# SS2D block on one Trainium2 core: the output stage with channels on partitions, norms and residuals by products on TensorE

## Chip, cores and metric

One NeuronCore of a Trainium2 chip. The time is the device time of one execution of the whole program, in microseconds (us).

## The reference

Four layers run one after the other on x of shape (8, 56, 56, 128) in float32. Layers 0, 2 and 3 are deformable convolutions with a small MLP; they are not touched. Layer 1 is a visual state-space block (SS2D). For each image, with Di = 256 inner channels and L = 56 x 56 = 3136 positions:

```python
xn = _ln(x, norm1_w, norm1_b)
xz = jnp.einsum('bhwc,ec->bhwe', xn, in_proj_w)
xx, z = jnp.split(xz, 2, axis=-1)
# xx: depthwise 3x3 convolution and silu; then a selective scan in four directions (K = 4, N = 16 states)
h = h * jnp.exp(dt_t[..., None] * A) + (dt_t * u_t)[..., None] * B_t[:, :, None, :]
# y: the sum of the four directions' outputs
y = _ln(y, out_norm_w, out_norm_b)
y = y * jax.nn.silu(z)
y = jnp.einsum('bhwd,cd->bhwc', y, out_proj_w)
x = x + y
xm = _ln(x, norm2_w, norm2_b)
h = jax.nn.gelu(jnp.einsum('bhwc,fc->bhwf', xm, fc1_w) + fc1_b)
x = x + jnp.einsum('bhwf,cf->bhwc', h, fc2_w) + fc2_b
```

`_ln` subtracts the mean over the channels, divides by the root of the variance plus 1e-5, and applies a weight and a bias for each channel. The lines from `y = _ln(...)` to the end are what the kernel calls the output stage.

## The kernel before

Class `Vss` computes layer 1. Its inner loop (`scans`) goes over 8 images, 4 directions in the order 1, 3, 0, 2, and 4 chunks of 784 positions: 128 steps. A step has 32 *units*; a unit holds 32 channels x 4 states on the 128 partitions and 784 positions on the free axis, so there are 4096 units. Each unit does the following:

- ACT: `decay`, the exponential dA (L1346), into one of two PSUM buffers.
- DVE: `inputs`, the product u of b and dtu (L1356) in three units of four; in the fourth, POOL does it as up (L1352). dtu is a copy of dt*x that PE spreads into PSUM (`spread`, L1340) once for each four units; it has one buffer.
- DVE: the scan itself (L1449), from dA and u to h.
- POOL: hc = h*c (L1454).
- PE: the sum of hc over the states into acc (L1378), opened at L1370 and closed by copies on ACT (L1389).

Beside the units two kinds of further work are emitted. `prepare` makes the next step's dt, b and c; one of its parts goes out every second unit. *Tasks* form a queue of generators: the input stage of the next image (norm, in-projection, nine-tap convolution as 18 products of 448 columns a chunk, seven chunks an image) and the output stages of an image, eight of them, each for SH = 392 positions. `advance(1)` runs the first task in the queue up to its next `yield`. It is called in 24 of 32 units (odd t, or t a multiple of 4), and in every unit while the last image is in its last direction. An output stage is queued when the last direction closes its chunk, two at a time. What is still queued after the last scan runs by itself; layer 2 follows it. `prepare`, the input stage and the output stage all take their PSUM from one bank, `misc`, with one buffer. Each engine works its own queue in order, and all loads and stores go through SP's queue.

The output stage before (L1159 to L1230, 28 yields) takes y with channels on partitions and goes over to positions on partitions: n = 98 positions in T = 4 groups.

- L1162 and L1164 load y (yin) and the gate sg, each 128 x 2 x 392.
- L1173: eight transposes on PE, two groups at a time. `stats` (L1062) takes BATCH_NORM_STATS2 (L1069) and BATCH_NORM_AGGREGATE (L1070) on DVE from PSUM; Ln and Exp (L204, L205) make the inverse root, and small ACT operations (L1073, L1074) the negated product with the mean. `normalize` (L1080) writes z on ACT.
- L1186: eight transposes back (L1090); ACT applies weight and bias as it copies to gT (L1187). POOL multiplies by sg (L1189).
- L1195: the projection, eight products with positions on the output's partitions. DVE adds the input rows xt (L1198).
- Statistics and normalization again, from xt; four transposes (L1090); ACT writes xT with weight and bias (L1208).
- fc1 (L1213), four products of 392 columns, each copied out by ACT with its bias (L1214); gelu with a table load ahead of it and one behind it (L1216, L1218); fc2 (L1224), 16 products on top of a bias row (L298).
- DVE adds xt (L1227); L1229 stores the rows.

A float32 product shows as two records of the profile on PE; a transpose shows as one.

Of the kernel before, what the change touches and what calls it, by code (L numbers as in the profile page):

```python
# [41 lines left out]
F32 = mybir.dt.float32  # L42
BF16 = mybir.dt.bfloat16
I32 = mybir.dt.int32
AF = mybir.ActivationFunctionType
# [5 lines left out]
NIMG, H, W, C = 8, 56, 56, 128  # L51
# [60 lines left out]
DI, NST, NDIR, RANK = 256, 16, 4, 8  # L112
NCH = DI // 128
XD = RANK + 2 * NST

LC = 448
# [4 lines left out]
SH = SC // 2  # L121

FF = 512
NF = FF // 128
# [16 lines left out]
def bcast(ap, axis, n):  # L141
    shape = list(ap.shape)
    shape.insert(axis, n)
    return ap.unsqueeze(axis).to_broadcast(shape)
# [845 lines left out]
class Vss:  # L990
# [27 lines left out]
    def weights(self):  # L1018
# [34 lines left out]

        w["sum"] = self.cp.tile([128, TC], F32, name="v_sum", tag="v_sum")
# [39 lines left out]
    def input_stage(self, i):  # L1094
# [34 lines left out]
        for c in range(NLC):  # L1129
# [7 lines left out]
            z = self.bg.tile([128, T, C], F32, name="z", tag="z", padded_shape=[128, T, DI])  # L1137
# [20 lines left out]

    def output_stage(self, i, c):  # L1159
# [7 lines left out]
        z = self.bg.tile([128, T, DI], F32, name="z", tag="z")  # L1167
        for t0 in range(0, T, 2):
            ps = self.misc()
            for t in range(2):  # L1170
                at = n * (t0 + t)
                for ch in range(NCH):
                    nc.tensor.transpose(ps[:n, DI * t + 128 * ch : DI * t + 128 * (ch + 1)], y[:, ch, at : at + n], self.net.ident)  # L1173
            yield
            yield
            srcs = [ps[:n, DI * t : DI * (t + 1)] for t in range(2)]
            rs = self.stats(srcs)
            yield
            self.normalize(z[:, t0 : t0 + 2], srcs, rs)
            yield  # L1180
        xt = self.bg.tile([128, T, C], F32, name="xt", tag="xt", bufs=2)
        nc.sync.dma_start(out=xt[:n], in_=self.rows_of(self.src[i], c, n))
        gT = self.bg.tile([128, NCH, m], F32, name="gT", tag="gT")
        for ch in range(NCH):
            ps = self.misc()
            self.transpose(ps, [z[:n, t, 128 * ch : 128 * (ch + 1)] for t in range(T)])  # L1186
            nc.scalar.activation(gT[:, ch, :], ps[:, :m], AF.Identity, bias=w["now_b"][:, ch : ch + 1], scale=w["now_w"][:, ch : ch + 1])  # L1187
            yield
        nc.gpsimd.tensor_mul(gT, gT, sg)  # L1189
        yield  # L1190
        yield
        po = self.misc()
        for t in range(T):
            for ch in range(NCH):
                nc.tensor.matmul(po[:n, 128 * t : 128 * (t + 1)], lhsT=gT[:, ch, n * t : n * (t + 1)], rhs=w["out"][:, ch, :], start=ch == 0, stop=ch == NCH - 1)  # L1195
        yield
        yield
        nc.vector.tensor_add(xt[:n], xt[:n], po[:n].rearrange("p (t c) -> p t c", c=128))  # L1198
        srcs = [xt[:n, t, :] for t in range(T)]
        rs = self.stats(srcs)  # L1200
        yield
        z = self.bg.tile([128, T, C], F32, name="z", tag="z", padded_shape=[128, T, DI])
        self.normalize(z, srcs, rs)
        yield
        ps = self.misc()
        self.transpose(ps, [z[:n, t, :] for t in range(T)])
        xT = self.bg.tile([128, m], F32, name="xT", tag="xT")
        nc.scalar.activation(xT, ps[:, :m], AF.Identity, bias=w["n2b"], scale=w["n2w"])  # L1208
        yield
        pre = self.bg.tile([128, NF, m], F32, name="pre", tag="pre", padded_shape=[128, NF, LC])  # L1210
# [11 lines left out]
        for t in range(T):  # L1222
            for f in range(NF):
                nc.tensor.matmul(po[:n, 128 * t : 128 * (t + 1)], lhsT=pre[:, f, n * t : n * (t + 1)], rhs=w["fc2"][:, f, :], start=False, stop=t == T - 1 and f == NF - 1)  # L1224
            if t % 2:
                yield
        nc.vector.tensor_add(xt[:n], xt[:n], po[:n].rearrange("p (t c) -> p t c", c=128))  # L1227
# [316 lines left out]
```

## Time and profile before

| | us |
|---|---|
| median of 3 runs | 18470.5 (18470.23 to 18477.48) |
| span of the profiled execution | 18479.8 |
| first to last scan (L1449) | 2365 to 13799 |
| last output stage ends | about 14015 |
| DVE busy | 15510.8 (84%) |
| POOL busy | 11801.5 (64%) |
| ACT busy | 11145.4 (60%) |
| PE busy | 13780.6 (75%) |

Of the profiled execution the trace gives its span and no other time. A row of a group of instructions reads: line, engine, operation, output<-input by the program's names, partitions x elements, count | busy us in all, mean ns of one | idle us of the engine just before them, and who ended that idle time. A row of a window gives, for each engine, its busy us and the number of its instructions in brackets, then the granted clock of TensorE as a share of full speed, the busy share of the DMA engines and GB/s. PEld is the load of weights, which runs beside PE. Matmuls are pipelined and their ends are modelled, so a busy PE is not a full one. A row of the timeline begins with its start and its length in us.

### The profile page before, as it was taken

How to read it: one execution, taken by the hardware profiler on the slowest of the kernel's cores; microseconds unless marked ns; L12 is line 12 of the kernel's file. 1: busy time of each engine (PE TensorE's matmuls, PEld its weight loads, DVE VectorE, ACT ScalarE, POOL GpSimd, SP SyncE). 2: the span in 40 equal slices, each digit the busy share in tenths (PEclk: the TensorE clock that was granted, in tenths of full speed). 3: DMA queues.
4: the chain of work that ended last, by engine and by line, in shares of the span. 5: the costliest groups of instructions: out<-in, count | busy, mean ns of one | idle time of the engine just before them, and what ended most of it. 6: DMA issues, size and time to landing. Idle time of an engine off the chain costs nothing. (4 is left out here: it accounts for less than half of the span.)

```text
span 18479.8 us, 257190 instructions
## 1 busy us (share of the span) xinstructions
PE 13780.6 (75%) x89795; PEld 6844.2 (37%) x89795; DVE 15510.8 (84%) x18797; ACT 11145.4 (60%) x20690; POOL 11801.5 (64%) x6462
## 2 busy tenths in 40 slices
PE   5777787678678778678778768767665888577777
PEld 4555422222222222222222222222224666455555
DVE  8888379988988988988988898898985887688886
ACT  4666565566566566566566656656554666456666
POOL 2221089998998998998998998899981111222221
PEclk7878888889889889889888888888886888677777
DMA  7777444444443444344343443443433777577777
GB/s 215 205 210 200 122 158 160 162 158 148 142 149 137 146 147 140 140 150 139 140 150 136 143 152 135 143 150 136 147 122 110 196 198 198 143 204 204 201 204 175
DMA packets 1341779, 2961.90 MB, mean 160 GB/s; under 512 B 91168, under 2 KB 892132, under 8 KB 1325836
## 3 DMA queue, kind: packets, MB, share of 16 engines
q1 hardware_dynamic: 1340460, 2945.21, 51.4%
q8 instruction: 718, 11.76, 0.3%
q14 instruction: 601, 4.92, 0.1%
HBM read 2243.88 MB, written 866.92 MB: 168 GB/s over the span
## 5 line engine op out<-in xcount | busy, mean ns | idle before, releaser
L1454 POOL TENSOR_TENSOR hc<-h,c 128x784 f32<-128x784 f32 x4096 | 7560.9, 1873 | 764.2 <-DVE h L1449 534.4
L1449 DVE TENSOR_TENSOR_SCAN h<-dA,st,u 128x784 f32<-128x784 f32 x3072 | 5569.9, 1838 | 316.2 <-ACT dA L1346 182.3
L1346 ACT ACTIVATE dA<-dt,v_A 128x784 f32<-128x784 f32 x4096 | 3742.8, 915 | 719.1 <-DVE h L1449 717.8
L1356 DVE TENSOR_TENSOR u<-dtu,b 128x784 f32<-128x784 f32 x3072 | 2875.7, 957 | 559.9 <-PE dtu L1340 555.5
L1378 PE MATMUL acc<-hc,v_sum 128*32 128x392 f32 x16384 | 3222.3, 552 | 105.8 <-POOL hc L1454 105.6
L1340 PE MATMUL dtu<-dt,ident 128*128 128x392 f32 x4096 | 2105.1, 642 | 1512.1 <-issue 1102.6
L736 POOL TENSOR_TENSOR ay<-hat,om 112x756 f32<-112x756 f32 (+2 forms) x192 | 525.8, 2738 | 2750.0 <-ACT hat L727 2346.6
L1449 DVE TENSOR_TENSOR_SCAN h<-dA,st,up 128x784 f32<-128x784 f32 x1024 | 1876.7, 1833 | 242.4 <-POOL hc L1454 176.7
L1352 POOL TENSOR_TENSOR up<-dt,b 128x784 f32<-128x784 f32 x1024 | 1900.3, 1856 | 132.1 <-DVE h L1449 110.8
L807 ACT COPY st<-pt 128x448 f32<-128x448 f32 (+1 forms) x2240 | 1177.8, 542 | 1216.4 <-PE pt L805 1210.1
L1452 ACT COPY st<-h 128x1 f32<-128x1 f32 x3072 | 581.7, 189 | 2159.0 <-DVE h L1449 2150.5
L1340 PEld LDWEIGHTS dtu<-dt,ident 128*128 128x128 f32 x4096 | 862.0, 235 | 2564.6 <-issue 1672.2
L775 DVE TENSOR_TENSOR win<-win,patch 112x252 f32 (+2 forms) x3456 | 1695.4, 503 | 124.4 <-DVE win L775 34.2
L805 PE MATMUL pt<-ident,sw 112*128 112x112 f32 (+2 forms) x8960 | 1609.7, 310 | 199.1 <-DMA sw<-skew 198.8
L1378 PEld LDWEIGHTS acc<-hc,v_sum 128*32 128x32 f32 x16384 | 769.8, 117 | 2488.2 <-issue 1675.4
L766 POOL MEMSET win<- 128x1820 f32 (+2 forms) x384 | 630.1, 1646 | 1466.2 <-DMA skew<-win 1159.6
L821 PE MATMUL yps<-st,xw 128*32 128x48 f32 (+5 forms) x35840 | 1077.7, 245 | 397.6 <-ACT st L807 394.8
L805 PEld LDWEIGHTS pt<-ident,sw 112*128 112x128 f32 (+2 forms) x8960 | 1119.5, 161 | 485.6 <-DMA sw<-skew 166.9
L772 DVE TENSOR_TENSOR patch<-ay,hat 112x756 f32<-112x756 f32 (+2 forms) x1152 | 1221.3, 1066 | 22.5 <-POOL ay L736 19.5
L821 PEld LDWEIGHTS yps<-st,xw 128*32 128x32 f32 (+2 forms) x35840 | 757.0, 126 | 825.9 <-ACT st L807 476.1
L1112 PE MATMUL misc<-xn,v_tap 128*128 128x448 f32 x2016 | 867.3, 574 | 96.5 <-ACT xn L1146 61.2
L725 ACT ACTIVATE hat<-om,taps 112x252 f32<-112x252 f32 x1280 | 755.7, 729 | 287.1 <-DVE patch L772 273.4
(165 smaller groups left out, 19517.2 us busy)
## 6 DMA issues: line engine op xcount, KB each, us to landing
dt<-dds SPq DMA_DIRECT2D x1024, 784.0 KB
b<-rows SPq DMA_DIRECT2D x512, 392.0 KB
c<-rows SPq DMA_DIRECT2D x512, 392.0 KB
dds<-dd SPq DMA_DIRECT2D x256, 784.0 KB
sw<-skew SPq DMA_DIRECT2D x224, 812.0 KB
sw<-skew SPq DMA_DIRECT2D x224, 672.0 KB
sw<-skew SPq DMA_DIRECT2D x224, 588.0 KB
xw<-table SPq DMA_DIRECT2D x224, 320.0 KB
```

What stands on the lines that cost most here:

```text
L772: nc.vector.tensor_mul(patch[:n], bcast(a, 3, KX), bcast(b, 2, KY))
L775: self.last_add = nc.vector.tensor_add(to, to, patch[:n, NCB * p : NCB * (p + 1)]).ins
L805: last = nc.tensor.transpose(ps[:m, n * g : n * (g + 1)], sw[:n, g, p : p + m], self.net.ident[:n, :n])
L807: nc.scalar.copy(st[:m], ps[:m, : G * n])
L821: self.nc.tensor.matmul(yps[CG * g : CG * (g + 1), t0:t1], lhsT=xw[:m, k + part, CG * g : CG * (g + 1)], rhs=st[:m, at + t0 : at + t1], st ...
L1340: last = nc.tensor.matmul(ps[:, b, :SH], lhsT=self.net.ident, rhs=s["dt", cg][:, 1, SH * b : SH * (b + 1)], start=True, stop=True)
L1346: nc.scalar.activation(da[:, :SC], s["dt", cg][:, 0], AF.Exp, scale=w["A"][:, k, NSG * cg + sg : NSG * cg + sg + 1])
L1352: nc.gpsimd.tensor_mul(u, s["dt", cg][:, 1], s["b", sg])
L1356: nc.vector.tensor_mul(halves[0], s["dtu", cg][:, :, :SH], halves[1])
L1378: nc.tensor.matmul(acc[r : r + TC, :SH], lhsT=w["sum"], rhs=hc[:, SH * b : SH * (b + 1)], start=False, stop=sg == NSG - 1)
L1449: nc.vector.tensor_tensor_scan(hh[:, ::step], dA[:, :SC][:, ::step], u[:, ::step], st[:, t : t + 1], ALU.mult, ALU.add)
L1454: nc.gpsimd.tensor_mul(hc, hh, s["c", sg])
```

## The change

The output stage keeps the channels on the partitions until fc2. No transpose is left in it.

- The first norm subtracts the mean by two products a half with I - J/256 and -J/256 (w["mid"], w["off"]; J is all ones), takes squares on ACT, and gets the variance, the same on all partitions, by products with J/256 (w["mean"]). Ln and Exp work in place in PSUM, on 128 x 392. DVE multiplies the two halves by that row.
- Weight and bias of the first norm go into the projection ahead of the loop: w["out"] is scaled by now_w, and a second matrix w["outb"] by now_b takes the gate sg by itself. The input rows xt are added in the same PSUM group by products with the identity.
- The second norm does the same with I - J/128 and J/128 (w["center"], w["mean1"]). Its weight goes into fc1 and its bias into fc1_b.
- The second residual, x, is added in fc2's PSUM group by products with the identity; ACT copies the result out.
- 24 yields instead of 28. z is 128 x 4 x 128 and no longer padded, gT is gone, yc and x are new, and `dynamic_dma_scratch_size` is 8192.

```diff
@@ -1051,6 +1051,22 @@
             nc.vector.tensor_scalar_mul(dg[:, ch, :], self.net.ident, ds[:, ch : ch + 1])
         w["skip"] = dg
 
+        for name, x, y in (("mean", 0.0, 1.0 / DI), ("off", 0.0, -1.0 / DI), ("mid", 1.0, -1.0 / DI), ("mean1", 0.0, 1.0 / C), ("center", 1.0, -1.0 / C)):
+            t = w[name] = self.cp.tile([128, 128], F32, name="v_" + name, tag="v_" + name)
+            if x:
+                nc.vector.tensor_scalar_add(t, self.net.ident, y)
+            else:
+                nc.vector.memset(t, y)
+        w["outb"] = self.cp.tile([128, NCH, 128], F32, name="v_outb", tag="v_outb")
+        for h in range(NCH):
+            nc.vector.tensor_scalar_mul(w["outb"][:, h, :], w["out"][:, h, :], w["now_b"][:, h : h + 1])
+            nc.vector.tensor_scalar_mul(w["out"][:, h, :], w["out"][:, h, :], w["now_w"][:, h : h + 1])
+        ps = self.misc()
+        for f in range(NF):
+            nc.tensor.matmul(ps[:, f : f + 1], lhsT=w["fc1"][:, 128 * f : 128 * (f + 1)], rhs=w["n2b"], start=True, stop=True)
+        nc.vector.tensor_add(w["fc1_b"], w["fc1_b"], ps[:, :NF])
+        nc.vector.tensor_scalar_mul(w["fc1"], w["fc1"], w["n2w"])
+
         w["sum"] = self.cp.tile([128, TC], F32, name="v_sum", tag="v_sum")
         nc.vector.tensor_reduce(w["sum"], self.net.ident.rearrange("p (c s) -> p c s", s=TS), AX.X, ALU.add)
 
@@ -1134,7 +1150,7 @@
             srcs = [xt[:n, t, :] for t in range(T)]
             rs = self.stats(srcs)
             yield
-            z = self.bg.tile([128, T, C], F32, name="z", tag="z", padded_shape=[128, T, DI])
+            z = self.bg.tile([128, T, C], F32, name="z", tag="z")
             self.normalize(z, srcs, rs)
             yield
             ps = self.misc()
@@ -1156,6 +1172,13 @@
 
 
 
+    def inverse_root(self, ps, squares, mean):
+
+        nc, m = self.nc, SH
+        for x, sq in enumerate(squares):
+            nc.tensor.matmul(ps[:, :m], lhsT=mean, rhs=sq, start=x == 0, stop=x == len(squares) - 1)
+        self.net.rsqrt(ps[:, :m], ps[:, :m], 128)
+
     def output_stage(self, i, c):
         nc, w, n, T, m = self.nc, self.w, SH // self.NT, self.NT, SH
         y = self.bg.tile([128, NCH, m], F32, name="yin", tag="yin")
@@ -1164,50 +1187,49 @@
         nc.sync.dma_start(out=sg, in_=self.gates[i][:, NCH:, m * c : m * (c + 1)])
         yield
         yield
-        z = self.bg.tile([128, T, DI], F32, name="z", tag="z")
-        for t0 in range(0, T, 2):
+        yc = self.bg.tile([128, NCH, m], F32, name="yc", tag="yc")
+        for h in range(NCH):
             ps = self.misc()
-            for t in range(2):
-                at = n * (t0 + t)
-                for ch in range(NCH):
-                    nc.tensor.transpose(ps[:n, DI * t + 128 * ch : DI * t + 128 * (ch + 1)], y[:, ch, at : at + n], self.net.ident)
-            yield
-            yield
-            srcs = [ps[:n, DI * t : DI * (t + 1)] for t in range(2)]
-            rs = self.stats(srcs)
-            yield
-            self.normalize(z[:, t0 : t0 + 2], srcs, rs)
-            yield
+            for g in range(NCH):
+                nc.tensor.matmul(ps[:, :m], lhsT=w["mid"] if g == h else w["off"], rhs=y[:, g, :], start=g == 0, stop=g == NCH - 1)
+            nc.scalar.copy(yc[:, h, :], ps[:, :m])
+            yield
+        nc.scalar.activation(y, yc, AF.Square)
+        yield
+        ps = self.misc()
+        self.inverse_root(ps, [y[:, h, :] for h in range(NCH)], w["mean"])
+        yield
+        yield
+        nc.vector.tensor_mul(yc, yc, bcast(ps[:, :m], 1, NCH))
         xt = self.bg.tile([128, T, C], F32, name="xt", tag="xt", bufs=2)
         nc.sync.dma_start(out=xt[:n], in_=self.rows_of(self.src[i], c, n))
-        gT = self.bg.tile([128, NCH, m], F32, name="gT", tag="gT")
-        for ch in range(NCH):
-            ps = self.misc()
-            self.transpose(ps, [z[:n, t, 128 * ch : 128 * (ch + 1)] for t in range(T)])
-            nc.scalar.activation(gT[:, ch, :], ps[:, :m], AF.Identity, bias=w["now_b"][:, ch : ch + 1], scale=w["now_w"][:, ch : ch + 1])
-            yield
-        nc.gpsimd.tensor_mul(gT, gT, sg)
-        yield
-        yield
-        po = self.misc()
+        yield
+        nc.gpsimd.tensor_mul(y, yc, sg)
+        yield
+        yield
+        ps = self.misc()
+        for h in range(NCH):
+            nc.tensor.matmul(ps[:, :m], lhsT=w["outb"][:, h, :], rhs=sg[:, h, :], start=h == 0, stop=False)
         for t in range(T):
-            for ch in range(NCH):
-                nc.tensor.matmul(po[:n, 128 * t : 128 * (t + 1)], lhsT=gT[:, ch, n * t : n * (t + 1)], rhs=w["out"][:, ch, :], start=ch == 0, stop=ch == NCH - 1)
-        yield
-        yield
-        nc.vector.tensor_add(xt[:n], xt[:n], po[:n].rearrange("p (t c) -> p t c", c=128))
-        srcs = [xt[:n, t, :] for t in range(T)]
-        rs = self.stats(srcs)
-        yield
-        z = self.bg.tile([128, T, C], F32, name="z", tag="z", padded_shape=[128, T, DI])
-        self.normalize(z, srcs, rs)
-        yield
+            nc.tensor.matmul(ps[:, n * t : n * (t + 1)], lhsT=xt[:n, t, :], rhs=self.net.ident[:n, :n], start=False, stop=False)
+        for h in range(NCH):
+            nc.tensor.matmul(ps[:, :m], lhsT=w["out"][:, h, :], rhs=y[:, h, :], start=False, stop=h == NCH - 1)
+        x = self.bg.tile([128, m], F32, name="x", tag="x")
+        nc.scalar.copy(x, ps[:, :m])
+        yield
+        xT = self.bg.tile([128, m], F32, name="xT", tag="xT")
+        pre = self.bg.tile([128, NF, m], F32, name="pre", tag="pre", padded_shape=[128, NF, LC])
         ps = self.misc()
-        self.transpose(ps, [z[:n, t, :] for t in range(T)])
-        xT = self.bg.tile([128, m], F32, name="xT", tag="xT")
-        nc.scalar.activation(xT, ps[:, :m], AF.Identity, bias=w["n2b"], scale=w["n2w"])
-        yield
-        pre = self.bg.tile([128, NF, m], F32, name="pre", tag="pre", padded_shape=[128, NF, LC])
+        nc.tensor.matmul(ps[:, :m], lhsT=w["center"], rhs=x, start=True, stop=True)
+        nc.scalar.copy(xT, ps[:, :m])
+        nc.scalar.activation(pre[:, 0, :], xT, AF.Square)
+        yield
+        ps = self.misc()
+        self.inverse_root(ps, [pre[:, 0, :]], w["mean1"])
+        yield
+        yield
+        nc.vector.tensor_mul(xT, xT, ps[:, :m])
+        yield
         for f in range(NF):
             ps = self.misc()
             nc.tensor.matmul(ps[:, :m], lhsT=w["fc1"][:, 128 * f : 128 * (f + 1)], rhs=xT, start=True, stop=True)
@@ -1220,11 +1242,12 @@
         po = self.misc()
         self.net.bias_row(po, n, w["fc2_b"], T)
         for t in range(T):
+            nc.tensor.matmul(po[:n, 128 * t : 128 * (t + 1)], lhsT=x[:, n * t : n * (t + 1)], rhs=self.net.ident, start=False, stop=False)
             for f in range(NF):
                 nc.tensor.matmul(po[:n, 128 * t : 128 * (t + 1)], lhsT=pre[:, f, n * t : n * (t + 1)], rhs=w["fc2"][:, f, :], start=False, stop=t == T - 1 and f == NF - 1)
             if t % 2:
                 yield
-        nc.vector.tensor_add(xt[:n], xt[:n], po[:n].rearrange("p (t c) -> p t c", c=128))
+        nc.scalar.copy(xt[:n], po[:n].rearrange("p (t c) -> p t c", c=128))
         yield
         nc.sync.dma_start(out=self.rows_of(self.dst[i], c, n), in_=xt[:n])
         yield
@@ -1534,7 +1557,7 @@
     from concourse.bass_utils import run_bass_kernel_spmd
 
     d = laid_out(inputs)
-    nc = bacc.Bacc("TRN2", target_bir_lowering=False, num_devices=1)
+    nc = bacc.Bacc("TRN2", target_bir_lowering=False, num_devices=1, dynamic_dma_scratch_size=8192)
     aps = {k: nc.dram_tensor(f"in_{k}", v.shape, mybir.dt.from_np(v.dtype), kind="ExternalInput").ap() for k, v in d.items()}
     out = nc.dram_tensor("out_x", (NIMG, L, C), F32, kind="ExternalOutput").ap()
     with tile.TileContext(nc) as tc:
```

More of the change, by code (lines that the diff above doesn't have):

```diff
@@ L1196, in output_stage @@
+        nc.scalar.copy(xT, ps[:, :m])
+        nc.scalar.activation(pre[:, 0, :], xT, AF.Square)
+        yield
+        ps = self.misc()
+        self.inverse_root(ps, [pre[:, 0, :]], w["mean1"])
         yield
         yield
-        nc.vector.tensor_add(xt[:n], xt[:n], po[:n].rearrange("p (t c) -> p t c", c=128))
-        srcs = [xt[:n, t, :] for t in range(T)]
-        rs = self.stats(srcs)
+        nc.vector.tensor_mul(xT, xT, ps[:, :m])
         yield
-        z = self.bg.tile([128, T, C], F32, name="z", tag="z", padded_shape=[128, T, DI])
@@ L1203, in output_stage @@
-        self.normalize(z, srcs, rs)
-        yield
-        ps = self.misc()
-        self.transpose(ps, [z[:n, t, :] for t in range(T)])
-        xT = self.bg.tile([128, m], F32, name="xT", tag="xT")
-        nc.scalar.activation(xT, ps[:, :m], AF.Identity, bias=w["n2b"], scale=w["n2w"])
-        yield
-        pre = self.bg.tile([128, NF, m], F32, name="pre", tag="pre", padded_shape=[128, NF, LC])
         for f in range(NF):
```

## Prediction

> **What bounds the kernel now.** The page's 40 slices show the changed layer as the stretch in which POOL and DVE stand at 8 and 9 tenths together; the rows of the scan (L1449) place it from 2365 to 13799 us, with a tail to 14015 us in which only output stages run. I then read the busy time by windows, one window for each kind of background work: convolutions, output stages, next to none, and the tail.
>
> ```profile
> core 0: us, PE busy (x) PEld busy (x) DVE busy (x) ACT busy (x) POOL busy (x), PEclk, DMA share, GB/s
> 5600.00:5950.00 350.00, 302.54 (x957) 103.93 (x958) 291.51 (x245) 226.53 (x395) 297.88 (x168) 0.92 0.40 138
> 12300.00:12900.00 600.00, 462.55 (x1712) 166.85 (x1712) 533.40 (x468) 376.81 (x697) 543.50 (x298) 0.84 0.42 146
> 13000.00:13500.00 500.00, 321.33 (x1194) 98.56 (x1190) 472.52 (x340) 271.07 (x468) 490.13 (x271) 0.82 0.40 142
> 13810.00:14010.00 200.00, 109.99 (x359) 67.03 (x360) 20.17 (x81) 75.94 (x162) 13.96 (x9) 0.58 0.10 29
> ```
>
> Without background (third row) POOL is busy 98% and DVE 95%. With output stages (second) both fall to about 90% and neither is full: time goes into waits. By the counts of hc (L1454) a scan unit takes about 2.85 us there, 2.97 with convolutions. The 4096 units take 11432 us; the units of 59.25 output stages (some 2170) and 49 convolution chunks (980) at those rates leave 2.5 for the rest. An output stage has 28 yields, 24 of 32 units advance one, so it lies over 37.3 units and costs 37.3 x 0.345 = 12.9 us. What these are made of stands in the DVE groups of the output window:
>
> ```profile
> L1449 DVE TENSOR_TENSOR_SCAN h<-dA,st,u 128x784 f32<-128x784 f32 x157 | 284.6, 1838 | 18.6 <-ACT dA L1346 12.6 <-POOL hc L1454 2.2 <-issue 1.0
> L1356 DVE TENSOR_TENSOR u<-dtu,b 128x784 f32<-128x784 f32 x158 | 148.8, 957 | 26.8 <-PE dtu L1340 26.5
> L1449 DVE TENSOR_TENSOR_SCAN h<-dA,st,up 128x784 f32<-128x784 f32 x53 | 97.2, 1833 | 10.1 <-POOL hc L1454 5.2 <-ACT dA L1346 4.9
> L1069 DVE BATCH_NORM_STATS2 bn_st<-misc 98x6 f32<-98x256 f32 x20 | 7.9, 416 | 3.6 <-PE misc L1173 3.6
> L1070 DVE BATCH_NORM_AGGREGATE bn_mv<-bn_st 98x2 f32<-98x6 f32 x44 | 7.3, 169 | 0.0
> L1069 DVE BATCH_NORM_STATS2 bn_st<-xt 98x6 f32<-98x128 f32 x24 | 5.8, 270 | 0.0
> L1227 DVE TENSOR_TENSOR xt<-xt,misc 98x512 f32<-98x512 f32 x6 | 4.1, 681 | 1.9 <-PE misc L1224 1.9
> L1198 DVE TENSOR_TENSOR xt<-xt,misc 98x512 f32<-98x512 f32 x6 | 4.1, 680 | 5.7 <-PE misc L1195 5.7
> ```
>
> About 5.65 stages and 211 units lie in it. The largest wait is not for the norms: it is u for dtu, PE's copy of dt (26.5 us, 0.126 a unit). Then the scan waits for dA (17.5). With convolutions, where PE has most to do, the same wait is twice as long a unit (31.1 us over 117 units; 27.7 and 29.5 in two like windows: 0.275); without background it is 0.5 us in 500:
>
> ```profile
> L1356 DVE TENSOR_TENSOR u<-dtu,b 128x784 f32<-128x784 f32 x88 | 82.3, 959 | 31.1 <-PE dtu L1340 30.7
> ```
> ```profile
> L1356 DVE TENSOR_TENSOR u<-dtu,b 128x784 f32<-128x784 f32 x145 | 134.4, 955 | 0.5 <-PE dtu L1340 0.5
> ```
>
> **The change, a stage at a time.** *DVE.* Out: 4 statistics of 256 (0.416), 4 of 128 (0.270), 8 aggregates (0.168), 2 additions (0.681): 5.45 us busy. In the timeline they start closer together than they last (a statistic and its aggregate every 0.26 us), some 0.08 less each: 4.0 us of DVE's time. In: yc by a PSUM row, 784 elements, like u (0.957), and xT, 392 (half of it and the fixed part, 0.51): 1.3 net. **-2.7 us.**
>
> *PE.* Out: 8 transposes of y (4 in 0.65), 12 of z (4 in 0.56), 16 records of the projection (14 in 3.31): 6.6 us. In: twelve products of 392 columns (four for the mean, two and one for the variances, two for the bias through sg, two projections, one to center), each two records in float32, by dtu's 4 records in 1.58 us: 9.5. Residuals: 4 of xt (8 records at 0.14) and 4 of x (8 at 0.163): 2.4. Sum +5.3 on the 16 us it now has (160.7 busy in misc less 70.5 of prepare, over 5.65 stages): 21.2. With 24 yields a stage lies over 32 units, so PE's extra work a unit goes from 0.43 to 0.66; convolutions have 0.97 (114 us over 117 units). On the line between (0.43, 0.126) and (0.97, 0.275) dtu's wait is 0.19 a unit: 6.1 a stage instead of 4.7. **+1.4 us.** Its bounds: unchanged (0), since the added work is spread over seven yields; and the rate of the convolutions, 8.8 (+4.1).
>
> *ACT.* Out: three roots (0.50 each), eight products (0.283), three negations (0.20), normalizing 4 x 0.559 + 4 x 0.482, gT 2 x 0.676, xT 0.673: 10.5. In: five copies (0.48, the last 0.58), squares (0.855, 0.48), two Ln and Exp on 392 (0.58 + 0.49): 6.0. ACT gives back 4.5 of 17; the longest block, the gelu with its two table loads (1.28 + 1.51 + 1.28), stays. The wait for dA is 3.1 a stage; in proportion -0.8, nothing if that block causes it: **-0.4**.
>
> *New waits on DVE.* Each new multiplication stands in DVE's queue, ahead of scans and u, behind product, Ln and Exp: 1.6 + 0.58 + 0.49, some 2.8 us. Two yields, 7.5 us, cover it. The waits it replaces were 96 us over 59 stages in the scan (45.4 for transposed y, 30.7 and 19.9 at the additions), 1.6 a stage. L1198 had the same cover behind 3.6 us of PE and waited 0.52; I take 0.7 each, **-0.2**, between -1.6 and, at L1198's longest wait of 3.9 each, +6.2.
>
> *Unit waits.* DVE idles some 0.1 a unit without any background, and for hc 0.035; over 5.3 fewer units the first is counted less against the stage (+0.5), the second less too (-0.2): **+0.3**. POOL's product is the same (1.85) before and after. Loads stay three a stage on SP's queue. yin's buffer is now held until the projection instead of the transposes; half a stage is left to land 392 KB. xt is needed three yields after its load, not six, some 11 us: at nothing while that covers it; if not, PE stands still with dtu behind it, a price inside +4.1.
>
> Sum -2.7 + 1.4 - 0.4 - 0.2 + 0.3 = **-1.6 us a stage, x 59.25 = -95 us.**
>
> *The tail.* The last image advances in every unit: 91 yields are done when its scans end, 3.25 stages of 28, so 4.75 are left, 43 us each (transposes at 13885.8, 13928.4, 13971.8). Of 24, 3.79 are done and 4.21 left.
>
> ```profile
> 13910.15 1.67 PE L1213 MATMUL misc<-xT,v_fc 128*128 128x392 f32 x2 [0.77 <-ACT xT L1208]
> 13911.86 0.59 ACT L1214 ACTIVATE pre<-misc,v_col 128x392 f32<-128x392 f32 x1 [1.76 <-PE misc L1213]
> ```
>
> Here a product of 392 costs 1.67 against 0.79 in the scan; the new serial chain, step by step, gives 51 us with all products at 1.67 and 39 at 0.79. I take 46: 4.21 x 46 = 194 instead of 204, and 0.54 stages more inside the scan (+6): **-4**. Bounds -40 and +16. Weights: some ten small DVE operations (0.28 for a 128x128) and four small products before the first stage: **+3**, or 0.
>
> [...]
>
> Total -95 - 4 + 3 = -96. The profiled execution spans 18479.8 us, 9 above the median of the runs shown; nothing else of it is timed. Off the median: **18375 us**.
>
> **Rivals.** (1) *The stalls go with DVE's work.* DVE and ACT are freer, so dtu's wait does not grow (0), dA's falls by 1.2 and the new multiplications wait 0.6 in all (-1.0): -4.9 x 59.25 = -290, **18180**. For it: DVE near 90% and ACT's 4.5 us. Against: the greatest wait is for PE. POOL doesn't forbid it: 2.71 a unit is still above the 2.58 without background.
> (2) *PE becomes the bound.* dtu waits at the convolutions' rate: +4.1 instead of +1.4, so +1.1 a stage, +65 in all, **18535**. It decides from 7.7 us of that wait a stage, 0.24 a unit. For: convolution windows with DVE emptier and units longer. Against: their bursts are six records of 448 in every yield.
> (3) *Given back at the new multiplications.* Each waits 1.5 instead of 0.7: nothing is left, **18470**. Against: the cover.
> (4) *Square needs a table of its own.* Two loads at each of two squares, 4 x 1.283 us of ACT a stage: dA's wait doubles (+3.1), +89 and 22 in the tail, **18580**. No row shows a Square. [...]
>
> **How the numbers follow.** Forecast 0.42 (18300 to 18433), rival 1 0.22, rival 3 0.17, rival 2 0.16, rival 4 0.03. Two tenths of a per cent, 37 us, is about what a measurement of this kernel tells from no change. Faster 0.64, same 0.17, slower 0.19. The range takes in rival 1 with a warmer tail (-320) and rival 2: 18150 to 18545.
>
> **What would show it.** The 98-row statistics vanish from DVE; u's idle time for dtu (560 us in all) rises by about 80 if right, by 240 under rival 2, not at all under rival 1; the two multiplications show 0.7 us of idle each; new ACT_TABLE_LOAD rows beyond 64 + 64 mean rival 4; the tail shrinks from 215 us to about 205. A tail much shorter, or units in output windows above 2.85 us, would make the prediction wrong.

## The result and the profile after

The changed kernel takes 18205.7 us (median of 4, 18201.4 to 18208.6) beside 18474.0 for the kernel before on the same chip (18470.2 to 18485.5): a ratio of 0.9851 (95% interval 0.9837 to 0.9865, below in brackets), 268 us less. The forecast was 96 less; the direction was right, the size 2.8 times too small. The profiled execution spans 18199.9 us, 279.9 below that of before. Of these the scan stretch of layer 1 gives 229 (11434.5 to 11205.6, first scan to the end of the last) and the tail 48 (214.6 to 166.5); the set-up ahead is 6 longer, the rest of the program 9 shorter.

The busy time by windows, of after, in an output stretch and in the tail (the columns are those of the first fence of the prediction):

```profile
core 0: us, PE busy (x) PEld busy (x) DVE busy (x) ACT busy (x) POOL busy (x), PEclk, DMA share, GB/s
12050.00:12650.00 600.00, 509.88 (x1859) 183.25 (x1857) 545.04 (x398) 391.03 (x657) 567.30 (x311) 0.92 0.44 151
13580.00:13740.00 160.00, 112.80 (x359) 61.63 (x356) 6.13 (x8) 56.28 (x80) 12.51 (x8) 0.77 0.13 38
```

In 600 us of output stages PE is busy for 510 instead of 463, and POOL, whose busy time goes with the units done, for 567 instead of 544: by the count of scans a unit takes 2.73 us instead of 2.86. The clock went from 0.84 to 0.92, in the tail from 0.58 to 0.77. DVE's groups in that window:

```profile
L1472 DVE TENSOR_TENSOR_SCAN h<-dA,st,u 128x784 f32<-128x784 f32 x165 | 299.7, 1838 | 13.3 <-ACT dA L1369 7.6 <-POOL hc L1477 1.2 <-ACT dd L1289 0.5
L1379 DVE TENSOR_TENSOR u<-dtu,b 128x784 f32<-128x784 f32 x164 | 154.3, 958 | 26.4 <-PE dtu L1363 25.5
L1472 DVE TENSOR_TENSOR_SCAN h<-dA,st,up 128x784 f32<-128x784 f32 x55 | 101.0, 1836 | 12.8 <-POOL hc L1477 9.7 <-ACT st L1475 2.9
L1203 DVE TENSOR_TENSOR yc<-yc,misc 128x784 f32<-128x784 f32 x7 | 6.6, 946 | 0.0
L1231 DVE TENSOR_TENSOR xT<-xT,misc 128x392 f32<-128x392 f32 x7 | 3.8, 548 | 2.4 <-ACT misc L205 2.4
```

The 98-row statistics and both additions are gone. yc's product waits for nothing, xT's 0.34 us. And dtu's wait, to which the forecast gave the largest loss, is 25.5 us over 219 units, 0.116 a unit, less than the 0.126 of before, though PE does more.

DVE's waits over the whole scan stretch, before (what waited, for what: us in all, times, longest):

```profile
DVE u L1356 <- PE dtu L1340: 473.5, 258, 7.8
DVE h L1449 <- ACT dA L1346: 234.3, 199, 4.2
DVE h L1449 <- POOL hc L1454: 214.4, 165, 3.2
DVE bn_st L1069 <- PE misc L1173: 45.4, 29, 2.6
DVE bn_st L1069 <- DMA xt<-x: 36.6, 7, 6.3
DVE xt L1198 <- PE misc L1195: 30.7, 22, 3.9
DVE xt L1227 <- PE misc L1224: 19.9, 24, 1.7
DVE h L1449 <- issue: 16.6, 12, 2.4
DVE h L1449 <- ACT st L1452: 12.7, 17, 2.6
```

and after:

```profile
DVE u L1379 <- PE dtu L1363: 460.6, 223, 7.8
DVE h L1472 <- POOL hc L1477: 265.3, 228, 3.1
DVE h L1472 <- ACT dA L1369: 164.9, 170, 4.5
DVE h L1472 <- ACT st L1475: 37.8, 32, 2.6
DVE xT L1231 <- ACT misc L205: 22.9, 17, 2.2
```

The same stretch as one window, before and then after:

```profile
2365.90:13800.40 11434.50, 8638.06 (x31300) 3030.12 (x31298) 10264.60 (x8601) 7051.73 (x13027) 10454.00 (x5761) 0.86 0.41 145
```
```profile
2371.50:13577.10 11205.60, 8848.54 (x31559) 3065.95 (x31558) 10138.81 (x7655) 6920.09 (x12073) 10451.48 (x5763) 0.89 0.42 148
```

DVE's busy time falls by 126; its idle time (length less busy time) falls by 103, from 1169.9 to 1066.8. The idle part: the waits of the statistics and additions that went (45.4, 30.7 and 19.9, together 96) became 24 at the two products, -72; dA -69; loads of xt for the input stage's statistics -33; issue (idle time for which the profile shows no cause) -16; dtu -13; against it hc +51, st +25 (ACT's copy of a scan's last value, from which the same unit of the next step starts) and small waits below the rows some +23.

The tail, DVE's timeline in after: the yc products stand 37.6 to 37.9 us apart, where the forecast had 46 a stage.

```profile
13601.35 0.97 DVE L1203 TENSOR_TENSOR yc<-yc,misc 128x784 f32<-128x784 f32 x1 [24.34 <-ACT misc L205]
...
13639.22 0.97 DVE L1203 TENSOR_TENSOR yc<-yc,misc 128x784 f32<-128x784 f32 x1 [27.77 <-ACT misc L205]
...
13676.94 0.97 DVE L1203 TENSOR_TENSOR yc<-yc,misc 128x784 f32<-128x784 f32 x1 [27.63 <-ACT misc L205]
```

### The profile page after: what moved, and what is told of

Its sections match the earlier page's. It is cut to its first block, busy times and chain, and to the rows that moved or that the text cites. A ratio compares the mean times of both kernels' runs of the same rounds, so it can differ in the third digit from the quotient of the medians.

```text
span 18199.9 us, 255839 instructions
## 1 busy us (share of the span) xinstructions
PE 13988.6 (77%) x90059; PEld 6876.1 (38%) x90059; DVE 15372.9 (84%) x17784; ACT 10987.6 (60%) x19646; POOL 11803.5 (65%) x6462
## 5 line engine op out<-in xcount | busy, mean ns | idle before, releaser
L1369 ACT ACTIVATE dA<-dt,v_A 128x784 f32<-128x784 f32 x4096 | 3745.5, 915 | 817.4 <-DVE h L1472 813.6
L1379 DVE TENSOR_TENSOR u<-dtu,b 128x784 f32<-128x784 f32 x3072 | 2868.9, 956 | 551.9 <-PE dtu L1363 541.1
L1363 PE MATMUL dtu<-dt,ident 128*128 128x392 f32 x4096 | 2037.5, 624 | 1317.1 <-issue 935.8
```

The lines of the kernel that those rows point to most:

```text
L1363: last = nc.tensor.matmul(ps[:, b, :SH], lhsT=self.net.ident, rhs=s["dt", cg][:, 1, SH * b : SH * (b + 1)], start=True, stop=True)
L1369: nc.scalar.activation(da[:, :SC], s["dt", cg][:, 0], AF.Exp, scale=w["A"][:, k, NSG * cg + sg : NSG * cg + sg + 1])
L1379: nc.vector.tensor_mul(halves[0], s["dtu", cg][:, :, :SH], halves[1])
```

## The experiments

The theories at the start: **W**, the time goes with DVE's work and own waits, and PE's products lie free beside them (this is rival 1); **K**, the higher granted clock did it; **Y**, the number of yields did it, since a stage of 24 lies over fewer units. Times are medians; "scan" is the scan stretch of the profiled execution. The runs come from several chips, on which the kernel before took 18466 to 18488 us: each ratio is to before on the run's own chip, and a plain difference between two runs carries some 20 us from that.

**1. DVE's statistics put back beside.** After, with eight statistics and eight aggregates more a stage on DVE.

```
+    def idle_stats(self, srcs):
+        for i, s in enumerate(srcs):
+            self.nc.vector.bn_stats(st[:, i, :], s)
+            self.nc.vector.bn_aggr(mv[:, i, :], st[:, i, :])
...
+        self.idle_stats([yc[:, h, 128 * k : 128 * k + 256] for h in range(NCH) for k in range(2)])
...
+        self.idle_stats([xT[:, 88 * k : 88 * k + 128] for k in range(4)])
```

> The changed kernel, with statistics put back on DVE beside the new work: behind the first multiplication four statistics of 256 columns of yc and their aggregates, behind the second four of 128 columns of xT; nobody reads them, the result stays. That is 4.1 us busy a stage by the old rows (0.416, 0.270, 0.168), some 2.9 net. Theory W (DVE's work set the time; PE's products were free): 2.9 x 60, about +170, near 18375 us. Rival K (the higher granted clock of TensorE did it): up to +40, near 18225. Rival Y (a stage lies over fewer units): 0, 18206.

Measured: 18354.0, ratio to before 0.9927 [0.991, 0.9943], +148 on after.

```profile
2370.10:13722.00 11351.90, 8938.91 (x31572) 3061.56 (x31570) 10290.66 (x8615) 6921.71 (x12074) 10457.32 (x5762) 0.87 0.42 146
```

DVE has 152 us more than in after, and the scan is 146 longer: DVE's work costs its own time, here one to one. The idle total stays (1061 us), though its parts change (dtu 382, dA 282); with later runs in view, in which that total moves by over 100 us without any change of work, that it stayed is one case. W holds for DVE's part.

**2. Before, with float32 products in place of its 20 transposes a stage.**

```
-                    nc.tensor.transpose(ps[:n, DI * t + 128 * ch : DI * t + 128 * (ch + 1)], y[:, ch, at : at + n], self.net.ident)
+                    nc.tensor.matmul(ps[:n, DI * t + 128 * ch : DI * t + 128 * (ch + 1)], lhsT=y[:, ch, at : at + n], rhs=self.net.ident, start=True, stop=True)
```

> The kernel before, with the output stage's 20 transposes made float32 products with the identity: 20 more records on PE, DVE and ACT as before. W: scan time within 40 us of the kernel before, the tail some 20 shorter if its clock rises, 18420 to 18510. K: granted clock in output windows at 0.90 or more instead of 0.84, and 100 us or more gained, 18370 or less. Y: 18470.

Measured: 18539.3, ratio 1.0029 [1.0016, 1.0041], above all that was expected: the scan is 15 us longer than before's and the tail 21. The clock in the window 12300 to 12900 is 0.86 (0.84 in before), in the tail 0.59 (0.58). K falls in the form that transposes keep the clock down; the third row of the prediction's first fence, 0.82 in a window without a transpose, spoke against it already. Replacing them moved the clock by 0.01 to 0.02, with 1781 records on PE in that window for 1712 (463.96 us busy for 462.55). After's clock, 0.92 and 0.77, came with longer products (128x392 for 98x98 and 128x128) and more records (1859 in 600 us); run 5, with more products and the transposes kept, has 0.62 in the tail.

**3. After, with four more yields, 28 as before.** One more behind each Square, one behind the projection's copy and one behind xT's product:

```
         nc.scalar.activation(y, yc, AF.Square)
         yield
+        yield
...
         nc.scalar.copy(x, ps[:, :m])
         yield
+        yield
...
         nc.vector.tensor_mul(xT, xT, ps[:, :m])
         yield
+        yield
```

> The changed kernel with four more yields, 28 as before: a stage lies over 37.3 units again. W: the scan as in the changed kernel, the tail 0.54 stage longer (38 us each, +20), 18225. K: 18206 to 18250. Y: the gain in the scan goes, +95 or more, 18300 and above.

Measured: 18301.7, ratio 0.9898 [0.9881, 0.9914]; scan 11284.1, +78 on after. Y seems borne out; it did not stay so.

```profile
2369.90:13654.00 11284.10, 8893.85 (x31554) 3117.26 (x31552) 10134.86 (x7654) 6880.62 (x12038) 10431.75 (x5763) 0.88 0.42 147
```

This run and before have the same number of yields, so they show the instructions alone, in one pattern of places. The profiled execution is 172 us shorter than before's. Of these DVE's busy time in the scan gives 130 and the tail 38 (176.9 us); DVE's idle time in the scan is only 21 less (1149 to 1170), with dtu at 513 (473.5 before), hc at 257 (214) and dA at 212 (234); set-up and the other layers are 17 longer. The products wait for under 2 us, so the 96 us of the old ones are gone, but other waits took most of their place.

**4. After, without the table preload behind the gelu.**

```
-        last = nc.scalar.activation(pre, pre, AF.Gelu_apprx_tanh)
-        with self.tc.issue_after(last.ins):
-            nc.scalar.preload_act_table_set(EXP_LN)
+        nc.scalar.activation(pre, pre, AF.Gelu_apprx_tanh)
```

> The changed kernel without the table load that is asked for behind gelu: the next Exp gets its own. The changed kernel has 44 loads at dA beside the 64 asked for. All theories: 64 loads instead of 108 in that place, 44 x 1.28 = 56 us of ACT less; by W 0 to 40 us gained, 18166 to 18206, as dA's wait still stands at 165 us in the scan; K and Y: 0.

Measured: 18523.1, ratio 1.0018 [1.0009, 1.0028]; every expectation was missed. ACT's groups show why:

```profile
L1367 ACT ACT_TABLE_LOAD x276 | 354.1, 1283 | 3.7
...
L1290 ACT ACT_TABLE_LOAD x157 | 201.4, 1283 | 2.8
L204 ACT ACT_TABLE_LOAD x150 | 192.4, 1283 | 16.7 <-DMA w_ln<-in_w_ln 12.3 <-PE misc L1179 1.7
...
L205 ACT ACT_TABLE_LOAD x53 | 68.0, 1283 | 0.9
```

Without the explicit set, a load is put before the exponentials (L1367, L205) and another before the logarithms (L1290, L204): ACT has 701 us more in the scan, the scan is 297 longer, and dA's wait is 434 us. With it, after has no load at L204, L205 or L1290 between the first scan and the end of the tail, only those of L1138, L1140, L1238 and L1240 and the 44 at L1369.

**5. Before, with PE's extra work alone.** Seven constant products of 392 columns a stage, each into the PSUM tile that the stage uses next, overwritten there.

```
+            for _ in range(2):
+                nc.tensor.matmul(ps[:, :m], lhsT=self.net.ident, rhs=w["fc1"][:, :m], start=True, stop=True)
```

> The kernel before, with seven constant 392-column products more in each output stage, each written into the PSUM tile that the stage uses next: PE gets about 5.3 us more a stage (16 to 21.3), and no other engine gets anything. The theory of the forecast (the wait of u for dtu follows PE's work) expects that wait up by 1.4 x 59.25 = 83 us in the scan stretch, and the whole at +80 to +100 us with the tail. The theory that DVE's work and the density of the stage set the time, and PE's products lie free in PE's own waiting, expects 0 to +25 us. The theory that more PE work raises the granted clock and so shortens the rest expects -30 or lower.

Measured: 18534.6, ratio 1.0032 [1.002, 1.0045], +59 (worked out from the ratio); scan +33, the tail most of the rest.

```profile
DVE u L1360 <- PE dtu L1344: 511.9, 282, 7.8
DVE h L1453 <- ACT dA L1350: 250.8, 202, 4.9
```
```profile
2364.10:13831.20 11467.10, 8836.61 (x32130) 3154.54 (x32128) 10277.36 (x8601) 7041.29 (x13027) 10440.35 (x5762) 0.88 0.42 145
```

PE's busy time in the scan rises by 199 us, about what the change brought (210), and dtu's wait by 38, not 83 (run 3, with after's products at the same 28 yields, has +40). PE's products are not free, but cost under half of the term. The granted clock over the scan is 0.88, where before has 0.86 and after 0.89, and the kernel is slower: the higher clock came without a gain here, and no run shows K as a cause.

**6. After, with ACT's give-back taken away.** Six copies of 392 columns and nine of one a stage, in three places.

```
+        for _ in range(2):
+            self.nc.scalar.copy(s, self.w["fc1"][:, :SH])
+        for _ in range(3):
+            self.nc.scalar.copy(s[:, :1], self.w["fc1"][:, :1])
```

> The kernel after, with about 4.5 us of copies added to each output stage on ACT (the work that the change had taken off it), read by nobody. The forecast priced the give-back at 0.4 a stage: +25 us. The theory that ACT's time is worth about half of itself here, as the run without the preload seemed to say (0.46 us for each us of table loads): +100 to +125 us. The theory that DVE's work alone sets the time, ACT's being hidden: 0 to +10 us. In the first two dA's wait of h (165 us in after) rises by the amount given; a raised number of table loads would blur the run.

Measured: 18219.7, ratio 0.9862 [0.9846, 0.9879], beside 0.9851 for after. ACT has 143 us more in the scan, about the 132 by which the change had lowered its busy time; the scan is 6 us shorter. At these places ACT's time is hidden; in run 4 it cost 0.42 us for each us, where the loads stood directly ahead of dA.

**7. After, with 20 yields.** One yield fewer behind each inverse root, behind POOL's product and behind xT's product.

```
         self.inverse_root(ps, [y[:, h, :] for h in range(NCH)], w["mean"])
         yield
-        yield
...
         nc.gpsimd.tensor_mul(y, yc, sg)
         yield
-        yield
...
         self.inverse_root(ps, [pre[:, 0, :]], w["mean1"])
         yield
-        yield
         nc.vector.tensor_mul(xT, xT, ps[:, :m])
-        yield
```

> The kernel after with four of the stage's 24 yields left out (one behind each inverse root, one behind the POOL product, one behind xT's product), so that a stage is 20 units. The theory that the number of units sets a part of the time, because a stage that ends sooner is denser and the tail starts with less left: -50 to -80 us in the scan stretch, the mirror of the four added ones. The rival, that the two yields behind the roots hide the 0.7 us each that DVE would otherwise wait for PSUM: the multiplications' own waits rise from 24 us to about 80, and the whole is 0 to +60 us.

Measured: 18292.7, ratio 0.9905 [0.9888, 0.9921]; scan +111 on after. A gain was expected and did not come; nor do the two products wait, 0.5 us in all, so the rival's reason is out too.

**8. After, with four empty yields at the head.**

```
         nc.sync.dma_start(out=sg, in_=self.gates[i][:, NCH:, m * c : m * (c + 1)])
         yield
         yield
+        yield
+        yield
+        yield
+        yield
```

> The kernel after with four yields added in one place, behind the loads at the head of the output stage, where no work is: the work of a stage is as dense as in after, and only its number of units is that of the run with 28 yields spread (+79 us in the scan stretch, +96 in all). The theory that the number of units counts expects about the same: +70 to +100. The theory that the place of the yields among the work counts (which instruction stands next to which unit of the scan) expects 0 to +30, of which about 20 in the tail.

Measured: 18289.1, ratio 0.9902 [0.9886, 0.9919]; scan +57 (in the profiled execution, which at 18255 was the fastest of the four). Fewer and more yields are both slower, and it matters little where they stand. Y as "fewer is better" is out.

What sets 24 apart: 24 of 32 units advance a task, so a stage of 24 yields is one step long, and the next starts at the same unit of its step. I counted the scans on DVE up to each yc product. In after the first six of an image's eight stages have it behind scan 15, 15, 16, 15, 15, 15 of their step; in run 3, with 28 yields, behind 15, 21, 26, 30, and 2 and 10 of the second step after. `prepare` puts its parts at the same units of every step. So 24 yields lay the stage's parts beside the same parts of `prepare` each time. Theory **P** (place): that place in the step moves the time.

**9 to 11. After, started later in the step.** Once an image (not the last), a task of 6, 12 or 18 empty yields goes ahead of the output stages:

```
+    def pause(self, count):
+        for _ in range(count):
+            yield
...
+                if k == 2 and c == NSC - 1 and i < self.images - 1:
+                    tasks.append(self.pause(6))
```

> The kernel after, with a task of six empty yields queued once an image ahead of its first output stage (not for the last image), so that every later task of that image stands 6 advances, 8 units, later in the step of 32 units; work, yields of a stage and tail are those of after. With 24 yields a stage is exactly one step long, so in after six of the eight output stages of an image start at the same unit of the step (the scans counted on DVE show yc's product at unit 12 to 16 in each), while with 28 or 20 yields, and in the kernel before, the start wanders by 4 to 6 units a stage. The theory that this fixed place in the step is worth the 60 to 110 us by which the runs with 28 and 20 yields are longer in the scan stretch expects the three runs with the place shifted to differ from after and from each other by tens of us, and their mean to lie near +60 to +100 in the scan stretch. The rival, that the place does not count and the other runs lost to something else, expects all three within 15 us of after.

> As the run with six empty yields, with twelve: the stages stand 16 units, half a step, later. The theory of the place: +40 to +150 us in the scan stretch against after, the farthest from after's place. The rival: within 15 us of after.

> As the run with six empty yields, with eighteen: 24 units later. The theory of the place: a value of its own, 0 to +150 us in the scan stretch. The rival: within 15 us of after.

**12. Before, with 24 yields**: one of each pair left out, four in all (the first stands in a loop of two).

```
             yield
-            yield
             srcs = [ps[:n, DI * t : DI * (t + 1)] for t in range(2)]
...
         nc.gpsimd.tensor_mul(gT, gT, sg)
         yield
-        yield
...
         yield
-        yield
         nc.vector.tensor_add(xt[:n], xt[:n], po[:n].rearrange("p (t c) -> p t c", c=128))
```

> The kernel before with four yields left out of each output stage (one of each pair: twice behind the transposes of y, once behind POOL's product, once behind the projection), so that its stage too is 24 yields and one step long, and the tail starts with about as many stages left as in after. The theory of the place expects a part of the change's gain from this alone, -30 to -100 us with about -25 of it in the tail, if the place that after got is good for this stage too. The rival, that the change's gain comes from its instructions alone, expects the tail's -25 and, in the scan stretch, nothing or a loss: the statistics and additions wait longer on DVE because a yield that covered them is gone (+20 to +60).

Measured, with the runs that followed:

| kernel | empty yields | us | ratio to before | scan us | DVE idle us | of it for dtu |
| --- | --- | --- | --- | --- | --- | --- |
| after | 0 | 18205.7 | 0.9851 [0.9837, 0.9865] | 11205.6 | 1067 | 460.6 |
| after | 6 | 18242.9 | 0.9873 [0.9856, 0.9889] | 11234.7 | 1094 | 415.0 |
| after | 12 | 18043.6 | 0.9764 [0.9747, 0.9780] | 11043.4 | 906 | 344.2 |
| after | 13 | 18202.5 | 0.9856 [0.9840, 0.9873] | 11207.9 | 1080 | 420.9 |
| after | 18 | 18173.7 | 0.9832 [0.9815, 0.9848] | 11164.6 | 1043 | 448.0 |
| before, 24 yields | 0 | 18298.6 | 0.9901 [0.9884, 0.9917] | 11287.5 | 1013 | 313.0 |
| before, 24 yields | 6 | 18505.7 | 1.0020 [1.0010, 1.0030] | 11498.5 | 1221 | 679.2 |
| before, 24 yields | 12 | 18391.9 | 0.9957 [0.9940, 0.9973] | 11372.4 | 1094 | 419.0 |
| before, 24 yields | 18 | 18487.1 | 1.0015 [1.0005, 1.0024] | 11471.8 | 1197 | 491.9 |

DVE is busy in the scan for 10121 to 10141 us in the rows of after and for 10275 to 10278 in the others; from row to row only its idle time moves.

The rival of runs 9 to 11 (all within 15 us) is out: +37, -162, -32, with the same instructions. Their mean is below after, though, not above as expected: after's own place is no lucky one. The place is not moved evenly, though: with twelve empty yields the first yc product of an image still stands behind scan 14 of its step, and the next five behind 30, so the order in the engines' queues is not that of the yields alone. With twelve the kernel beats both: 18043.6, 162 below after. Its waits show a fall at dtu and hc and none at dA:

```profile
DVE u L1383 <- PE dtu L1367: 344.2, 196, 7.8
DVE h L1478 <- POOL hc L1483: 214.2, 195, 2.5
DVE h L1478 <- ACT dA L1373: 164.5, 204, 3.5
DVE h L1478 <- POOL up L1379: 55.8, 36, 1.8
```

Run 12 gained 183 (0.9901) with no instruction changed, more than it was given. That raised the question how much of the change's gain was the place.

**13 to 15. Before, with 24 yields, started later in the step**, with the pause of runs 9 to 11:

```
+                if k == 2 and c == NSC - 1 and i < self.images - 1:
+                    tasks.append(self.pause(6))
```

> The kernel before with 24 yields, with a task of six empty yields queued once an image ahead of its first output stage (not for the last image). After's instructions at four places took 18205.7, 18242.9, 18043.6 and 18173.7, a mean of 18166. If the instructions alone are worth what the forecast said, about -96, the kernel before with 24 yields has a mean of some 18260 over its four places (18299 at the first); if they are worth the 166 to 188 us by which the two kernels of 28 yields differ, the mean is some 18340, and its first place was a lucky one. This run by itself: 18200 to 18400.

> As the run before it, with twelve: one more of the four places. The theory of the forecast's size needs this and its neighbours to average about 18250, the other about 18355. If the best place is set by the units and prepare alone, and not by the stage's own instructions, this one is the lowest of the four, as with after (there -162).

> As the runs before it, with eighteen: the last of the four places. The same two means are told apart: about 18250 over the three new places, or about 18355.

Run 12's first place was the lucky one: the four times average 18421, above both values that run 13 set against each other (18260 and 18340). The lowest of the four is the first, not that with twelve, so the best place is not set by the units and `prepare` alone. The four ratios average 0.9973 for the old instructions and 0.9830 for the new, 1.43% or 264 us apart; at 28 yields (runs 3 and 8 against before) it is 1.0%, some 185. The four places scatter by about 90 to 100 us round either mean, which leaves some 65 on that difference, so the two agree. The instructions alone are worth some 185 to 265 us. The 24 yields by themselves gave 50 on the average of places (0.9973), of which a part is the shorter tail.

Run 13 shows what a place is. Its work is run 12's; dtu's wait is 313 there and 679 here:

```profile
DVE u L1353 <- PE dtu L1337: 313.0, 176, 7.8
```
```profile
DVE u L1357 <- PE dtu L1341: 679.2, 341, 7.7
```

In its timeline, DVE's u waits by the same 3.76 us one step (94.7 us) later:

```profile
12473.80 1.85 DVE L1357 TENSOR_TENSOR u<-dtu,b 128x784 f32<-128x784 f32 x2 [3.76 <-PE dtu L1341]
...
12568.48 1.86 DVE L1357 TENSOR_TENSOR u<-dtu,b 128x784 f32<-128x784 f32 x2 [3.76 <-PE dtu L1341]
```

and PE's queue ahead of the first of them reads

```profile
12468.53 1.62 PE L1252 MATMUL misc<-xb,v_xproj 128*40 128x392 f32 x2
12470.09 1.50 PE L1379 MATMUL acc<-hc,v_sum 128*32 128x392 f32 x6
12471.52 0.93 PE L1341 MATMUL dtu<-dt,ident 128*128 128x392 f32 x2
12472.28 0.82 PE L1214 MATMUL misc<-xT,v_fc 128*128 128x392 f32 x2
12472.94 0.82 PE L1341 MATMUL dtu<-dt,ident 128*128 128x392 f32 x2
```

A product of `prepare` (L1252), the sums (L1379) and dtu's two halves (L1341) stand back to back, with an fc1 product of the stage (L1214) between the halves. The same wait comes back one step on again, at 12663.57, and so do the smaller ones between. From first scan to first scan, the 42 steps that hold output stages and no convolution in all of these kernels (the last three of an image and the first three of the next) last 92.8 us in run 13, 87.5 in run 12, 88.0 in after and 85.9 in run 10. Times 42, the first two differ by 221 us, all of what run 13 lost to run 12 in the scan.

**16. After, with thirteen empty yields once an image.**

```
+                    tasks.append(self.pause(13))
```

> The kernel after with thirteen empty yields once an image, one more than at its best place so far (18043.6 with twelve). Three advances go to four units, so one yield more also moves each part of the stage to another of the three slots among four units, against dtu's spread, which goes out once in four. If the slot counts, this run differs from the one with twelve by over 40 us, and that with fifteen (the same slot as twelve) by less; if the place counts smoothly, all of 13, 14 and 15 lie between 18040 and 18175, rising.

Measured: 18202.5. One empty yield costs some 160 us, though yc's product stands behind the same scan as in run 10 (30 in the second stage of both). The idle time is 1080 against 906: dA 276 (164), dtu 421 (344), st 72 (16). By steps, the six of output stages from each image to the next give only 17 of the 164 us by which the scan is longer (515.3 to 517.8 us for the six). Steps 3 to 7, where the input stage of the following image comes out of the same queue behind them, give 122 (445.5 to 463.0). So the yield cost most where it moved the input stage, which theory P had left out. That the slot among the three advances counts is possible and not shown: fourteen and fifteen were not tried.

## Why the prediction was wrong in size

The scan's -229 and the tail's -48, by the forecast's own steps (a stage's value times 59.25):

- **The step that failed: dtu's wait, +1.4 a stage, +83 in all.** "On the line between (0.43, 0.126) and (0.97, 0.275) dtu's wait is 0.19 a unit." It is 0.116; over the scan it fell by 13. The step's PE work was right: 21.7 a stage by the output window, for 21.2 (its parts for the old work add to 6.8, not 6.6; nothing hangs on that). What failed is the line from that work to the wait. Run 5 prices PE's work alone at +38 in this wait and +33 in the scan, 0.6 a stage; runs 12 and 13 have it at 313 and 679 with the same work. The wait follows what stands beside dtu in PE's queue far more than how much PE does. Two windows with different stages are two sets of neighbours, not two points of a line.
- **New waits, -0.2: measured -1.2 (-72 us).** The old waits, 96 us, were counted rightly; the products were given 0.7 each and wait 0.01 and 0.4. The cover of two yields was enough, as the prediction said before it took L1198 as a measure. That this is a gain in the scan as a whole is not shown: run 3 has these waits gone too, and 21 us less idle time than before.
- **ACT, -0.4.** dA's wait fell by 69 (-1.2), rival 1's amount. Run 6 gives ACT's work back and loses nothing in the scan, so this fall is not shown to be ACT's 4.5 us; at other places of the same instructions dA's wait is 165 to 276.
- **DVE, -2.7: measured -2.1** (126), and run 1 shows that it counts in full. Right in kind, 34 us too large. Run 3 has it at 130.
- **Unit waits, +0.3.** hc took +51 and st +25; the input stage's loads of xt (-33) and issue (-16) had no term. The step saw that a stage of 24 lies over 32 units, a whole step, and priced only the five units fewer. That 24 fixes the stage's place was not seen; runs 9 to 16 have it at -162 to +37 about after, and 207 between two places of the old instructions. This uncertainty had no term in the sum.
- **The tail, -4: measured -48**, beyond the bound of -40 (which leaves out the +6 that the other bound has); a tail much shorter was one of the prediction's own signs of being wrong. A stage takes 37.7 us instead of 46, below even the 39 of the chain at 0.79, though fc1's products there still take 1.65 to 1.68: the chain was counted too long. The granted clock is 0.77 for 0.58; run 2, at 0.59, shows that it isn't the transposes' absence alone. The warmer tail in the forecast's range (-320 beside rival 1's -290, some 30 us) was the author's estimate; that a higher clock by itself gives this, no run shows: after's tail is 44 us below the -4, with the clock at 0.77 and fc1's products as slow as in before (1.67 to 1.68).
- **Setup, +3: measured +6**, which cannot be told from scatter: the first scan starts at 2350 to 2380 us in the runs here.

Rivals 2 and 4 are out: PE is not the bound, and no table load stands at either Square. Rival 1 (18180) came nearest, part by part: DVE's work in full, dtu +0, dA -1.2, own waits -1.0 against the measured -2.1, -0.2, -1.2, -1.2. DVE's part is shown by runs 1 and 3; that the waits agree as well is partly luck of the place, since the same instructions took 18044 to 18243 us over five places.

Still open: which meetings in the queues make the good place good, and how much of the 172 us missed is place. By the means the instructions account for 90 to 170 of it. At 28 yields what they gave is in the main DVE's work (130) and the tail (38), of 172 in all.

## What to carry to other kernels

When one generator is advanced in a fixed rhythm beside a loop, its length in yields against the loop's period decides whether its parts drift or lock; a locked one may gain or lose as much as the change itself (here 207 us between two places of the old instructions, beside the 185 to 265 that the new ones are worth), also in the work that follows in the same queue (122 us of run 16's 164), so compare two versions over several starting places before a difference of a per cent is put down to instructions. Price work added to a busy engine by a dummy copy of that work (run 5: +38 us of dtu's wait), not by a line through windows that hold other work (+83). Count the busy time that a change takes off the fullest engine in full (run 1: 152 us of it, 146 us of time); the waits of the instructions that went can come back at others, as in run 3 (96 us went, the idle time fell by 21).

## What was not expected of the hardware

Table loads of 1.283 us: after has 44 at L1369 beside the 64 + 64 expected, where a dA is scheduled between the gelu and the preload (as at 12126.87 us of after), and they do not go with the time (runs 10 and 16 have 7 each and differ by 159 us). Removing the preload put some 550 more loads into the layer, since there the exponentials (L1367, L205) and the logarithms (L1290, L204) were served by separate loads. And the granted clock rose by 0.08 in the output windows with the change (0.84 to 0.92), by 0.02 when only the transposes became products (0.86), and over the scan by 0.02 in run 5 (0.86 to 0.88), which was slower.
